# ScalarE moments, a wider row spacing and a shared c/d bank in a Winograd-tiled attention and FFN kernel

## The chip, the cores and the metric

The kernel runs on one core of a Trainium2 chip. Its engines run side by side, each with a queue of its own that is worked off in order: TensorE (PE, with PEld for its weight loads), VectorE (DVE), ScalarE (ACT), GpSimd (POOL) and SyncE (SP), whose queue issues nearly all DMAs. An instruction that has to wait for another engine holds up everything behind it in its queue. The metric is the time of one execution in microseconds (us) on the device; the time before is 2470.33 us, the median of three runs from 2461.07 to 2472.49.

## The reference

The input is x with 8 sequences of 512 rows of 1024 numbers, all float32. Two blocks follow each other, each with a layer norm in front of it and one behind it, and a residual sum:

```python
x = x + _layernorm(attn(_layernorm(x), Wq, Wk, Wv, Wo))       # causal attention, 16 heads of 64, rotary
x = x + _layernorm(ffn(_layernorm(x), weight, bias, lora_A, lora_B, starts))

def _layernorm(x, axis=-1, eps=1e-05):
    m = jnp.mean(x, axis=axis, keepdims=True)
    v = jnp.var(x, axis=axis, keepdims=True)
    return (x - m) / jnp.sqrt(v + eps)
```

`ffn` is one 1024 x 1024 linear layer with a low-rank adapter that is chosen for each sequence. So each sequence meets a projection with Wo, a norm of the result, the sum with x, a norm of that sum, the projection with the FFN weight, a norm and a sum.

## The kernel before

**Three stages.** The first (V) projects the eight sequences with Wv, the second does the query and key products and the attention, the third does sixteen projections: q = 0 to 7 are the eight sequences with Wo, q = 8 to 15 the same with the FFN weight. The first and third stages use one scheme, class `Group` and `products` (L295 to L391), and the change lies there.

**Tiling.** A matrix product is done by two nested levels of Strassen-Winograd: seven outer products P1 to P7 (`GROUPS`, in the order `ORDER`), each of seven inner products (`SUBS`, in the order `SLOTS`). An inner product is two matmuls of 128 x 128 by 128 x 256 in the code, and one inner product is one *tick*. A projection takes N2 = 49 ticks. The inner products of a group add into four accumulators in PSUM, named a, b, c and d, each 128 x 256 float32. `SLOTS` says in which order within a group: slot 0 opens b (P6), slot 1 opens a (P1), slot 2 adds the last product P3 of the *group before* into that group's c, slot 3 opens c (P5), slot 4 opens d (P4), slot 5 adds to b (P7), slot 6 adds to a (P2).

**Drains.** One tick after a product, its `drain` (L339) takes the results out: after slot 1, ACT copies a to `p1` (L347) and DVE forms `u2` from b and `p1`; after slot 5, DVE adds b into `p1` and adds c and d to it (three adds, L342); after slot 6, ACT copies a (L354); after slot 2, DVE adds c to `u2`. PE may add to b in slot 5 only when DVE has read it for `u2`, and `u2` needs ACT's copy. PE may add P3 to c in slot 2 of the next group only when DVE has read c.

**Buffers.** PSUM has eight banks. `ACCS` (L79) gives one, two, two and one buffers to a, b, c and d, with two for a when q >= 0; each buffer takes a bank of its own, though it fills half of one. In V two more banks hold transposes, in the third stage one holds the adapter's products.

**Order.** It is written out by hand. `at(tick, fn)` puts an event on a tick; `run` issues at each tick the product, then the drain of the product before, then the events of that tick in the order in which they were put there. With base = 49 q, the events of projection q at `base + k` that matter here are these. Sums of the outer products (L275 to L277): at k = 45 DVE adds A to U and at 46 U to c22 (one instruction of 128 x 1024 each), at 48 c22 to c12, at 52 A to c22; POOL adds to c21 at 38 and 47. Operands of the next projection (`plan_right`, L1167): loads of R11, R21, R12, R22 at 10, 17, 24, 31 on SP's queue, then T1 at 38, T2 at 45, T4 at 52 and T3 at 63 on POOL (three subtractions each); for q >= 8 T1 and T3 are DVE's.

**Rows.** `plan_rows` (L1203) treats the result of a projection in four row tiles t of 128 rows, seven ticks apart, starting at k = 55 + 7 t, that is during the next projection. For a tile: load the residual row (k); `stats` in four steps at k, k+1, k+3, k+4, which are `bn_stats` on the two halves and `bn_aggr` on DVE, a square root on ACT, reciprocal and the factor `nb` on DVE; two `norm` passes on ACT (k+6, k+7, L420); two adds of the residual on POOL (k+8, k+9, L1124); a store (k+14). For q < 8 the norm of the sum follows, with `stats` on DVE at k+14 to k+18 (key x), two `norm` passes at k+20 and k+21, two transposes on DVE at k+24 and k+25 (`turn_x1`, L1133) and eight small stores. Tiles 0 and 1 are c11 and c21, tiles 2 and 3 are c22 and c12. The residual rows take three buffers with tag `row` and one with tag `lb`; `lb` also holds the adapter's output matrix, which POOL fetches by an indirect DMA (`pick_b`, L1090).

Of the kernel before, what the change touches and what calls it, by code (L numbers as in the profile page):

```python
# [10 lines left out]
F32 = mybir.dt.float32  # L11
I32 = mybir.dt.int32
AF = mybir.ActivationFunctionType
# [4 lines left out]
P = 128  # L18
# [7 lines left out]
HALF = 512  # L26
# [37 lines left out]
SUB = 256  # L64
# [11 lines left out]
SLOTS = ["P6", "P1", "P3", "P5", "P4", "P7", "P2"]  # L76

QK = {"P1": "A", "P2": "B", "P6": "D", "P7": "E", "P4": "F", "P5": "D", "P3": "E"}
ACCS = {"a": 1, "b": 2, "c": 2, "d": 1}  # L79
SLOT_L = {"L11": 0, "L12": 1, "S3": 2, "L22": 3, "S1": 4, "S2": 5, "S4": 6}  # L80
SLOT_R = {"R11": 0, "R21": 1, "T3": 2, "R22": 3, "T1": 4, "T2": 5, "T4": 6}

# [51 lines left out]
def sandwich_kernel(  # L134
# [58 lines left out]
    def at(tick, fn, kind=None):  # L193
        events[tick].append((kind, fn) if kind else fn)
# [100 lines left out]
    class Group:  # L295
# [9 lines left out]
        def product(self, p):  # L305
            l, r, a = SUBS[p]
            first = a not in self.acc
            if first:
                self.acc[a] = env["acc"].tile(
                    [P, SUB], F32, tag=a, bufs=2 if a == "a" and self.q >= 0 else ACCS[a], name=f"acc{a}_{self.name}"  # L310
                )
            acc = self.acc[a]
            left, right = self.W[self.L], RX[self.q, self.R][:, SLOT_R[r]]
            for k in range(2):
                stays = right[:, k, :] if self.q < B else by_blocks(right, k)
                if self.q < 0:
                    moving = left[:, SLOT_L[l], k, :]
                else:
                    moving = left[:, 4 * k : 4 * k + 4, SLOT_L[l], :]
                nc.tensor.matmul(  # L320
                    acc, lhsT=stays, rhs=moving,
                    start=(first and k == 0), stop=True, skip_group_check=True,
                )
            if self.lora and p in LORA_SUB:
                half, cols = self.lora
                i, c = LORA_SUB[p]
                nc.tensor.matmul(
                    acc, lhsT=hts[self.q - B][:, cols[c], :],
                    rhs=env["lb"][self.q - B][:, half * HALF + i * SUB : half * HALF + (i + 1) * SUB],
                    start=False, stop=True, skip_group_check=True,  # L330
                )
# [7 lines left out]
        def drain(self, p):  # L339

            acc, t = self.acc, self.t
            add = lambda out, x, a: nc.vector.tensor_tensor(out, acc[a], x, op=ALU.add)  # L342
            if p == "P1":
                env["u2"].reverse()
                for n, pool in (("p1", env["p1"]), ("u2", env["u2"][0])):
                    t[n] = pool.tile([P, SUB], F32, tag=n, name=f"{n}_{self.name}")
                nc.scalar.copy(t["p1"], acc["a"])  # L347
                add(t["u2"], t["p1"], "b")
            elif p == "P7":
                add(t["p1"], t["p1"], "b")  # L350
                add(self.dest(1, 1), t["p1"], "c")
                add(self.dest(1, 0), t["p1"], "d")
            elif p == "P2":
                nc.scalar.copy(self.dest(0, 0), acc["a"])  # L354
            elif p == "P3":
                add(self.dest(0, 1), t["u2"], "c")
# [38 lines left out]
    def stats(key, srcs, step):  # L395
        small = env["small"]
        if step == 0:
            ln[key] = small.tile([P, 2, 6], F32, tag="bnst", name=f"bn_{key}")
        if step < 2:
            nc.vector.bn_stats(ln[key][:, step, :], srcs[step])  # L400
        if step == 1:
            mv = small.tile([P, 2], F32, tag="mv", name=f"mv_{key}")
            nc.vector.bn_aggr(mv, ln[key])
            ln[key] = mv
        if step == 2:
            mv = ln[key]
            sd = small.tile([P, 1], F32, tag="sd", name=f"sd_{key}")
            nc.scalar.activation(sd, mv[:, 1:2], AF.Sqrt, bias=eps, scale=1.0)
            ln[key] = mv, sd
        if step == 3:  # L410
            mv, sd = ln[key]
            rs = small.tile([P, 1], F32, tag="rstd", name=f"rstd_{key}")
            nc.vector.reciprocal(rs, sd)
            nb = small.tile([P, 1], F32, tag="nb", name=f"nb_{key}")
            nc.vector.tensor_scalar(nb, mv[:, 0:1], rs, -1.0, op0=ALU.mult, op1=ALU.mult)
            ln[key] = rs, nb

    def norm(key, dst, src):
# [647 lines left out]
    with ExitStack() as a:  # L1066
# [5 lines left out]
        ps_p = a.enter_context(tc.tile_pool(name="ps_p2", bufs=1, space=PSUM))  # L1072
        ps_t = a.enter_context(tc.tile_pool(name="ps_t2", bufs=1, space=PSUM))
        env.update(acc=ps_p, cp=cp, p1=tl, u2=[tl, tmp], small=small)

# [12 lines left out]
        def pick_b(b):  # L1090
            lb[b] = (rows if b % 2 else lc).tile([P, E], F32, tag="lb", bufs=1, name=f"lb_{b}")
            pick(lb[b], lora_b, 1, b)
# [19 lines left out]
        def load_row(q, t):  # L1112
            if (q, t) == (NQ - 1, 3):
                row[q, t] = lc.tile([P, E], F32, tag="lb", bufs=1, name=f"row_{q}_{t}")
            elif q < B and t == (3 if q + 1 < B else 0):
                row[q, t] = rows.tile([P, E], F32, tag="lb", bufs=1, name=f"row_{q}_{t}")
            else:
                row[q, t] = rows.tile([P, E], F32, tag="row", bufs=3, name=f"row_{q}_{t}")
            src = x[q, ts(t, P), :] if q < B else x1d[q - B][:, t, :]
            nc.sync.dma_start(out=row[q, t], in_=src)  # L1120
# [46 lines left out]
        def plan_right(q, base):  # L1167

            if q > 1:
                at(base + 6, next_roles)  # L1170
            for n, k in (("R11", 10), ("R21", 17), ("R12", 24), ("R22", 31)):
                if q == 1 and n != "R22":
                    continue
                at(base + k, lambda n=n: load_right(gp, q, n))
                if q >= B:
                    at(base + k + 4, lambda n=n: sub_right(q, n, nc.gpsimd, slice(0, 3)))
            if q >= B:
                for h, k in ((0, 25), (1, 39)):
                    at(base + k, lambda h=h: lora_in(q - B, h), "pe")
                    at(base + k, lambda ph, h=h: lora_keep(q - B, h, ph), "post")  # L1180
                    for g in range(2):
                        at(base + k, lambda n=f"R{g + 1}{h + 1}": sub_right(q, n, nc.vector if h else nc.gpsimd, slice(3, 4)))
                at(base + 42, lambda: sub_ht(q - B))
                if q - B:
                    at(base + (10 if q - B > 1 else 33), lambda: pick_b(q - B))
                if q + 1 < NQ:
                    at(base + 43, lambda: pick_a(q - B + 1))
            for n, k in (("T1", 40 if q == 1 or q >= B else 38), ("T2", 46 if q >= B else 45), ("T4", 52), ("T3", 63)):
                eng = nc.vector if q >= B and n in ("T1", "T3") else nc.gpsimd
                for m in range(3):  # L1190
                    at(
                        base + k + (m if eng is nc.vector else 0),
                        lambda n=n, m=m, eng=eng: sum_right(gp, q, n, eng, slice(m, m + 1)),
                    )
# [8 lines left out]
        def plan_rows(q, base):  # L1203

            for t in range(NT):
                k = base + 55 + 7 * t
                key = f"{'o' if q < B else 'y'}{q}_{t}"
                at(k, lambda t=t: load_row(q, t))
                for m in range(4):
                    at(k + m + m // 2, lambda t=t, m=m, key=key: stats(key, halves(q, t), m))  # L1210
                for h in range(2):
                    at(k + 6 + h, lambda t=t, h=h, key=key: norm(key, halves(q, t)[h], halves(q, t)[h]))
                    at(k + 8 + h, lambda t=t, h=h: add_row(q, t, h))
                at(k + 14, lambda t=t: store_rows(q, t))
                if q < B:
                    key = f"x{q}_{t}"
                    for m in range(4):
                        at(k + 14 + m + m // 2, lambda t=t, m=m, key=key: stats(key, halves(q, t), m))
                    for h in range(2):
                        at(k + 20 + h, lambda t=t, h=h, key=key: norm(  # L1220
                            key, row[q, t][:, ts(h, HALF)], halves(q, t)[h]
                        ))
                    for g in range(2):
                        at(k + 24 + g, lambda t=t, g=g: turn_x1(q, t, g))
                        at(k + 29 + g, lambda t=t, g=g: store_x1(q, t, g))
# [172 lines left out]
```

## Time and profile before

| what | value | how to read it |
|---|---|---|
| median of the runs | 2470.33 us | three runs, 2461.07 to 2472.49 |
| profiled execution | 2470.53 us | its own time |
| its span | 2468.4 us | first to last instruction |
| PE busy | 2356.1 us, 95% | so PE idles 112.3 us in all |
| DVE, ACT, POOL busy | 73%, 42%, 62% | averages over stages that differ |
| projections 1 to 5, mean length | 44.8 us | from 1749.9 to 1974.1 us, five of them, cut at their longest waits |
| of such a projection (1838.3 to 1883.3) | DVE 40.33, ACT 18.76, POOL 38.07 us busy | of 45.00 us |

The page has one line for each group of instructions: line of the code, engine, operation, output and input with their shapes, count, busy time and mean duration, then the idle time of the engine just before. The timeline gives for each instruction its start, its length, its engine and line, and in square brackets how long the engine had been idle and what released it.

### The profile page before, as it was taken

The numbers are of one execution on the slowest core, as the hardware profiler recorded it, in microseconds if no ns is written. First come the engines' busy times: TensorE is split into PE (matmuls) and PEld (weight loads), VectorE is DVE, ScalarE is ACT, GpSimd is POOL, SyncE is SP. The second block draws the span as 40 slices with busy tenths as digits, with TensorE's granted clock in tenths as the row PEclk, the third lists the DMA queues.
The fourth block names the chain that finished last, engine by engine and source line by source line (L and its number), as shares of the span: only waits on it lengthen the run. The fifth ranks groups of instructions, "written<-read, shape, count | busy, mean of one in ns | idle before, by whom it ended". The sixth has DMA issues, their size and how long they took to land.

```text
span 2468.4 us, 37185 instructions
## 1 busy us (share of the span) xinstructions
PE 2356.1 (95%) x11936; PEld 1858.0 (75%) x11936; DVE 1790.1 (73%) x3946; ACT 1045.4 (42%) x2650; POOL 1535.8 (62%) x1139
## 2 busy tenths in 40 slices
PE   6999999999999999999999999899999988999997
PEld 4887887886677777777777776558888867888886
DVE  8777767485857759577595866776899888776676
ACT  3323331025555555555555566652434433222223
POOL 4878875204363553735646364776887886777874
PEclk8999999999999999999999999899999999999999
DMA  7697787998899897989889897467777788545443
GB/s 264 196 302 247 245 269 230 353 304 265 269 298 291 248 340 239 312 297 292 314 259 341 265 303 245 135 230 261 241 213 233 216 261 246 136 144 148 139 122 119
DMA packets 506016, 606.47 MB, mean 246 GB/s; under 512 B 197600, under 2 KB 344032, under 8 KB 503264
## 3 DMA queue, kind: packets, MB, share of 16 engines
q1 hardware_dynamic: 504288, 598.87, 76.7%
q0 software_dynamic: 1536, 5.24, 0.7%
q8 instruction: 96, 1.57, 0.3%
q14 instruction: 96, 0.79, 0.1%
HBM read 371.20 MB, written 199.23 MB: 231 GB/s over the span
## 4 chain that ended last, share of the span: by engine, by line
PE 65%; DVE 6%; DMA 5%; POOL 2%; ACT 2%; issue 1%; SPq 1%; ACTq 0%; DVEq 0%; POOLq 0%
PE accb_q_P L641 7%; PE acca_q_P L641 7%; PE accc_q_P L641 7%; PE accc_P L320 6%; PE accb_P L320 6%; PE acca_P L320 6%; PE s L753 6%; PE po L835 6%; PE ptp L814 5%; PE accd_q_P L641 3%; PE accd_P L320 3%; DMA wo_d<-wc_wo 1%; DVE U L360 1%; ACT pr L784 1%; DMA attn<-opt 1%
## 5 line engine op out<-in xcount | busy, mean ns | idle before, releaser
L784 ACT ACTIVATE pr<-pr,nm 128x128 f32<-128x128 f32 (+3 forms) x512 | 281.0, 550 | 188.4 <-DVE nm L774 188.2
L800 ACT ACTIVATE pr<-pr,rs 128x128 f32<-128x128 f32 x470 | 231.0, 550 | 109.4 <-DVE rs L792 109.3
L774 DVE CUSTOM_DVE_ANT_0 pr<-s,mask 128x128 f32<-128x128 f32 (+3 forms) x512 | 224.2, 484 | 43.1 <-PE s L753 41.1
L641 PE MATMUL acca_q_P<-xs,ls 128*128 128x256 f32 x896 | 217.3, 385 | 0.8 <-DMA ls<-wqk 0.8
L641 PE MATMUL accc_q_P<-xs,ls 128*128 128x256 f32 x896 | 217.1, 385 | 0.0
L641 PE MATMUL accb_q_P<-xs,ls 128*128 128x256 f32 x896 | 216.3, 384 | 0.8 <-DVE u_q_P L117 0.8
L1124 POOL TENSOR_TENSOR c<-c,row 128x512 f32<-128x512 f32 x120 | 161.8, 1357 | 88.4 <-ACT c L420 73.2
L641 PEld LDWEIGHTS acca_q_P<-xs,ls 128*128 128x128 f32 x896 | 165.3, 190 | 49.9 <-issue 19.4
L641 PEld LDWEIGHTS accc_q_P<-xs,ls 128*128 128x128 f32 x896 | 165.3, 190 | 48.2 <-issue 20.2
L641 PEld LDWEIGHTS accb_q_P<-xs,ls 128*128 128x128 f32 x896 | 165.4, 190 | 44.9 <-issue 6.6
L753 PE MATMUL s<-qk 64*128 64x128 f32 (+3 forms) x1024 | 192.5, 472 | 4.4 <-DVE nm L774 4.2
L814 PE MATMUL ptp<-ident,pr 128*128 128x128 f32 x1280 | 178.7, 278 | 12.8 <-DVE nm L774 5.9
L814 PEld LDWEIGHTS ptp<-ident,pr 128*128 128x128 f32 x1280 | 147.6, 142 | 44.8 <-ACT pr L800 15.9
L275 POOL TENSOR_TENSOR T<-R,T 128x512 f32<-128x512 f32 (+1 forms) x96 | 171.3, 1812 | 14.2 <-PE accc_P L320 9.6
L567 POOL TENSOR_TENSOR wc_g<-wc_g 128x256 f32<-128x256 f32 (+1 forms) x120 | 127.0, 1077 | 79.6 <-DMA wc_g<-in_wqk_dram 76.3
L835 PE MATMUL po<-pT,v 128*64 128x512 f32 (+3 forms) x1024 | 157.6, 446 | 8.2 <-ACT pT L829 6.1
L835 PEld LDWEIGHTS po<-pT,v 128*64 128x64 f32 x1024 | 72.8, 138 | 100.1 <-issue 66.2
L684 POOL TENSOR_TENSOR B_q<-B_q,m 128x1024 f32<-128x1024 f32 x14 | 33.1, 2368 | 175.7 <-DVE B_q L681 175.7
L641 PE MATMUL accd_q_P<-xs,ls 128*128 128x256 f32 x448 | 108.8, 386 | 0.4 <-DVE p_q_P L117 0.4
L829 DVE COPY pT<-ptp 128x384 f32<-128x384 f32 (+1 forms) x132 | 80.4, 614 | 39.3 <-PE ptp L814 39.2
L753 PEld LDWEIGHTS s<-qk 64*128 64x128 f32 x1024 | 73.1, 186 | 44.7 <-issue 28.7
L567 POOL TENSOR_TENSOR wc_wo<-wc_wo 128x256 f32<-128x256 f32 (+1 forms) x64 | 66.0, 1049 | 64.2 <-DMA wc_wo<-in_wo_dram 50.8
(1120 smaller groups left out, 5750.6 us busy)
## 6 DMA issues: line engine op xcount, KB each, us to landing
ls<-wqk SPq DMA_DIRECT2D x392, 256.0 KB, 5.3
xs<-xop SPq DMA_DIRECT2D x392, 256.0 KB, 5.4
R<-attn SPq DMA_DIRECT2D x32, 896.0 KB, 6.4
wqk<-wc_g SPq DMA_DIRECT2D x16, 1568.0 KB, 9.4
x<-in_x_dram SPq DMA_DIRECT2D x32, 512.0 KB, 9.7
v<-vd SPq DMA_DIRECT2D x64, 256.0 KB, 5.4
attn<-ops SPq DMA_DIRECT2D x16, 1024.0 KB, 7.7
row<-in_x_dram SPq DMA_DIRECT2D x32, 512.0 KB, 5.4
```

What stands on the lines that cost most here:

```text
L275: eng.tensor_tensor(RX[q, n][:, c], RX[q, x][:, c], RX[q, y][:, c], op=ALU.subtract)
L320: nc.tensor.matmul(acc, lhsT=stays, rhs=moving, start=(first and k == 0), stop=True, skip_group_check=True,)
L567: eng.tensor_tensor(out, x, y, op=op)
L641: nc.tensor.matmul(acc[:, :, w, :], lhsT=ls[:, k, w, :], rhs=xs_[:, :, k, :], start=(first and w == 0 and k == 0), stop=True, skip_group_c ...
L753: nc.tensor.matmul(ps[:, j, at : at + L], lhsT=qT[r, qb], rhs=kT[r, : qb + 1], start=True, stop=True,)
L774: nc.vector.tensor_tensor_reduce(out=v[:, j, :], in0=self.ps[qb][:, j, :], in1=work2["mask"][:, S - L :], scale=-1.0 / HD**0.5, scalar=3.0e38,
L784: nc.scalar.activation(v[:, j, :], v[:, j, :], AF.Exp, bias=nm[:, j : j + 1], scale=-1.0, accum_out=sm[:, j : j + 1],)
L800: nc.scalar.mul(v, v, rs[:, j : j + 1])
L814: nc.tensor.transpose(pt[:, n, :], self.pr[qb][:, j, ts(kb, P)], ident)
L829: copy(self.pT[j][:, : qb + 1, ts(qb, P)], self.pt[j][:, : qb + 1, :])
L835: nc.tensor.matmul(po[j * HD : (j + 1) * HD, kb * P :], lhsT=self.v[:, kb, ts(j, HD)], rhs=self.pT[j][:, kb, kb * P :], start=(kb == 0), s ...
L1124: nc.gpsimd.tensor_tensor(c, c, row[q, t][:, ts(h, HALF)], op=ALU.add)
```

## The change

The moments (mean and variance) of the *first* norm behind the Wo projection (key o, q < 8) are no longer computed by `stats` on DVE but by a new function `moments`, by ACT passes whose elementwise results go to a spare PSUM bank called `unread` that nobody reads; only their running sums are used. The row tiles of q < 8 are nine ticks apart instead of seven. The accumulators c and d are two halves of one tile of one bank, with two buffers, and a has two buffers in every stage, V included. With this `first` is false for d, so only c's first matmul carries the start flag. In the drain after slot 5, d is read before c. For the last q < 8 the `lb` buffer goes to tile 1 instead of tile 0, and one fetch moves from tick 33 to 42.

```diff
-ACCS = {"a": 1, "b": 2, "c": 2, "d": 1}
...
-            if first:
-                self.acc[a] = env["acc"].tile(
-                    [P, SUB], F32, tag=a, bufs=2 if a == "a" and self.q >= 0 else ACCS[a], name=f"acc{a}_{self.name}"
-                )
+            if a in "ab" and first:
+                self.acc[a] = env["acc"].tile([P, SUB], F32, tag=a, bufs=2, name=f"acc{a}_{self.name}")
+            elif a == "c" and first:
+                both = env["acc"].tile([P, 2, SUB], F32, tag="c", bufs=2, name=f"accc_{self.name}")
+                self.acc["c"], self.acc["d"] = both[:, 0], both[:, 1]
...
             elif p == "P7":
                 add(t["p1"], t["p1"], "b")
+                add(self.dest(1, 0), t["p1"], "d")
                 add(self.dest(1, 1), t["p1"], "c")
-                add(self.dest(1, 0), t["p1"], "d")
...
+    def moments(key, srcs, junk, step):
+
+        small, act, n = env["small"], nc.scalar.activation, len(srcs)
+        if step == 0:
+            nm = small.tile([P, 2], F32, tag="nm", name=f"nm_{key}")
+            for i, v in enumerate(srcs):
+                act(junk[:, : v.shape[-1]], v, AF.Identity, scale=-1.0 / E, accum_out=nm[:, i : i + 1])
+            if n > 1:
+                act(nm[:, 0:1], nm[:, 0:1], AF.Identity, bias=nm[:, 1:2], scale=1.0)
+            ln[key] = nm
+        if step == 1:
+            sq = small.tile([P, 2], F32, tag="sq", name=f"sq_{key}")
+            for i, v in enumerate(srcs):
+                act(junk[:, : v.shape[-1]], v, AF.Square, bias=ln[key][:, 0:1], scale=1.0, accum_out=sq[:, i : i + 1])
+            ln[key] = ln[key], sq
+        if step == 2:
+            nm, sq = ln[key]
+            sd = small.tile([P, 1], F32, tag="sd", name=f"sd_{key}")
+            if n > 1:
+                act(sq[:, 1:2], sq[:, 1:2], AF.Identity, bias=eps, scale=1.0 / E)
+            act(sd, sq[:, 0:1], AF.Sqrt, bias=sq[:, 1:2] if n > 1 else eps, scale=1.0 / E)
+            ln[key] = nm, sd
+        if step == 3:
+            nm, sd = ln[key]
+            rs = small.tile([P, 1], F32, tag="rstd", name=f"rstd_{key}")
+            nc.vector.reciprocal(rs, sd)
+            nb = small.tile([P, 1], F32, tag="nb", name=f"nb_{key}")
+            act(nb, nm[:, 0:1], AF.Identity, scale=rs)
+            ln[key] = rs, nb
...
+        unread = ps_t.tile([P, HALF], F32, tag="unread", bufs=1, name="unread")
...
-            elif q < B and t == (3 if q + 1 < B else 0):
+            elif q < B and t == (3 if q + 1 < B else 1):
...
-                    at(base + (10 if q - B > 1 else 33), lambda: pick_b(q - B))
+                    at(base + (10 if q - B > 1 else 42), lambda: pick_b(q - B))
...
-                k = base + 55 + 7 * t
+                k = base + 55 + (9 if q < B else 7) * t
...
-                    at(k + m + m // 2, lambda t=t, m=m, key=key: stats(key, halves(q, t), m))
+                    at(k + m + m // 2, lambda t=t, m=m, key=key: (
+                        moments(key, halves(q, t), unread, m) if q < B else stats(key, halves(q, t), m)
+                    ))
```

## The prediction

> **What bounds the kernel now.** I read the page's slices first, then PE's waits, then the timelines of all engines around the longest of these waits.
>
> ```profile
> PE   6999999999999999999999999899999988999997
> ACT  3323331025555555555555566652434433222223
> ```
>
> PE is full nearly everywhere, ACT is the emptiest engine. Time can be won only where PE waits; here are all waits behind the first Wo projection that the change touches, and one of V's:
>
> ```profile
> PE accc_P L320 <- DVE A L342: 20.1, 9, 4.2
> PE accb_P L320 <- DVE u_P L342: 3.7, 2, 2.1
> PE acca_-6_P L320 <- ACT A_-6_1100 L354: 0.8, 1, 0.8
> ```
>
> Six of the nine waits for c are in projections 1 to 6, once in each: 11.0 us together, 1.83 us each. Two of 4.2 and 3.4 us are in q = 7 and 8, with both waits for u (2.1 and 1.6). The place, in PE's timeline (second line; the others are from V):
>
> ```profile
> 142.56 1.13 PE L320 MATMUL acca_-6_P<-wv_L,R_-6_839 128*128 128x256 f32 x4 [0.75 <-ACT A_-6_1100 L354]
> 145.62 0.66 PE L454 MATMUL ptx<-ident,x 128*128 128x128 f32 x4 [0.20 <-ACT x L420]
> ...
> 1794.18 1.13 PE L320 MATMUL accc_P<-wo_S,R 128*128 128x256 f32 x4 [1.94 <-DVE A L342]
> ```
>
> Products start 0.864 us apart (eleven from 1780.86 to 1790.36). The one at 1794.18 is tick 51 of its projection: P3 into c, which DVE must have read. DVE's own timeline shows why it has not:
>
> ```profile
> 1787.61 0.38 DVE L342 TENSOR_TENSOR U<-accc_P,u_P 128x256 f32<-128x256 f32 x1
> ...
> 1788.82 2.30 DVE L360 TENSOR_TENSOR U<-U,A 128x1024 f32<-128x1024 f32 x1
> 1791.16 2.17 DVE L360 TENSOR_TENSOR c<-c,U 128x1024 f32<-128x1024 f32 x1
> 1793.26 0.41 DVE L342 TENSOR_TENSOR p_P<-accb_P,p_P 128x256 f32<-128x256 f32 x1
> 1793.70 0.42 DVE L342 TENSOR_TENSOR A<-accc_P,p_P 128x256 f32<-128x256 f32 x1
> 1794.05 0.41 DVE L342 TENSOR_TENSOR A<-accd_P,p_P 128x256 f32<-128x256 f32 x1
> ...
> 1796.02 0.41 DVE L342 TENSOR_TENSOR u_P<-accb_P,p_P 128x256 f32<-128x256 f32 x1
> ```
>
> Between the last U drain (tick 45) and c stand two wide sums of 4.5 us. No `bn_stats` of key o is in this stretch: those that go were at ticks 55 to 80.
>
> **DVE at ticks 45 to 54.** A tile's relief is 2 x 0.67 + 0.21 + 0.21 = 1.8 us (`bn_stats`, `bn_aggr`, `nb`), 7 us for each projection, but elsewhere. What matters is what the nine-tick spacing puts here: tile 3's x statistics come at 47 and 48 (were 41, 42), tile 2's transposes at 48 and 49 (were 44, 45). I walk through DVE's new order, with distances between starts from the same timeline. The U drain now starts when its product ends, 1787.13, as no transpose is ahead of it. Then drain 0.46, U 2.34, c22 2.10, one `bn_stats` 0.60, b 0.44, d 0.35: c is read from 1793.42 to 1793.83, and PE resumes 0.06 later, at 1793.89. It could have at 1792.24: the wait is 1.65 instead of 1.94, in spite of d being read first, which costs 0.35. But u of the next group, which PE needs at tick 54, now stands behind a transpose (0.62), `bn_stats` (0.71), `bn_aggr` (0.12), the c12 sum (1.64) and a second transpose (0.62): it starts at 1793.76 + 3.71 = 1797.47 and ends at 1797.89. PE would be there at 1793.89 + 2.70 = 1796.59, so it waits 1.36 us. Sum 3.0 us a projection, against 1.83.
>
> **ACT.** The rows for a pass:
>
> ```profile
> L784 ACT ACTIVATION_READ_ACCUMULATOR pr<-pr,nm 128x1 f32 x512 | 95.9, 187 | 0.0
> L784 ACT ACTIVATE pr<-pr,nm 128x512 f32<-128x512 f32 x128 | 91.4, 714 | 139.6 <-DVE nm L774 139.4
> L420 ACT ACTIVATE c<-c,nb_o,rstd_o 128x512 f32<-128x512 f32 x64 | 49.9, 803 | 15.9 <-DVE nb_o L415 15.9
> L408 ACT ACTIVATE sd_o<-mv_o,eps 128x1 f32<-128x1 f32 x32 | 9.5, 296 | 12.6 <-DVE mv_o L403 12.6
> ```
>
> A running sum adds a read of 0.19, of which 0.09 stands out. A second operand by partition costs 0.09 (0.803 against 0.714), so Identity, which has none, is 0.62 + 0.09 and Square 0.71 + 0.09. All four passes of a tile write the same `unread`, so each waits for the one before to end: 0.03 more (the gap that dependent DVE instructions show). That makes 0.74 and 0.83; four small instructions of 0.33 follow. A tile is 2 x 0.74 + 2 x 0.83 + 4 x 0.33 = 4.5 us, and one root of 0.3 goes: 16.6 us more for each projection on an engine with 18.8 busy in 45: 79%. It fits on average. But ACT must also copy a (L347) on time: from slot 1 it has about 2.6 us until PE stops at slot 5. At 61 that just holds (0.15 us). From 61 to 89 nothing loosens the row of tiles 0 (norm), 1, 2 and 3: I add ACT's queue up from tile 3's old x norm at 1798.2. The copy before tick 61 ends at 1803.7; then tile 0's rest with its norms (to 1807.2), a copy, tile 1 with two copies (to 1814.1), tile 2 with tile 0's x norm (1.42) and copies (to 1822.7), tile 3 with tile 1's x norm (to 1828.8), the copy for group 5 to 1829.15, u to 1829.65. PE reaches that slot, tick 89, at 1804.2 + 28 x 0.864 = 1828.4. It waits 1.2 us. If a pass took only 0.60 and 0.70 and a small one 0.2 (no wait among them), 3.7 us less stand ahead of that copy, and nothing is late; at the norm's rate (0.803 + 0.12 for all) 2 us more are. So ACT costs 0 to 3.6 us a projection; I take 1.35, nearest to the rows of L784. The spare destination could make a pass shorter; no row shows it.
>
> By the Trainium skill, "ScalarE: Activation LUTs", section "What ACT_TABLE_LOAD costs", an immediate pass is 186 ns + 0.833 ns an element and each pointer operand adds 93 ns: 0.61 and 0.71 us, as the rows say. Its section "Rules for kernel authors" says to use VectorE, not ScalarE, for adds and multiplies; that speaks against the change: a half-row that took DVE 0.67 takes ACT 1.6. Were all of it on the path, 32 tiles x 2.4 would be 77 us; by the queues above only what is late counts.
>
> **POOL.**
>
> ```profile
> 1779.41 2.68 POOL L1124 TENSOR_TENSOR c<-c,row 128x512 f32<-128x512 f32 x2 [4.54 <-ACT c L420]
> 1782.05 4.30 POOL L275 TENSOR_TENSOR T<-R,R 128x512 f32<-128x512 f32 x3
> 1786.30 2.52 POOL L360 TENSOR_TENSOR c<-c,c 128x512 f32<-128x512 f32 x2
> 1788.76 6.25 POOL L275 TENSOR_TENSOR T<-R,T 128x512 f32<-128x512 f32 x3
> 1794.96 3.49 POOL L360 TENSOR_TENSOR c<-c,U 128x512 f32<-128x512 f32 x2
> 1798.42 5.26 POOL L275 TENSOR_TENSOR T<-R,T 128x512 f32<-128x512 f32 x3
> ```
>
> Tile 3's residual adds move from ticks 35, 36 to 41, 42, behind T1 and the first c21. T1 can't start before PE is through tick 37 (1781.0), which frees its buffer, so POOL's stretch to the end of T4 becomes 4.25 + 2.46 + 2.64 + 6.20 + 3.46 + 5.23 = 24.24 and ends at 1805.3. PE wants T4 at tick 63, now 1805.9. So the adds are just covered, by PE's own waits: without them PE would be there at 1802.6 and wait 2.7 us for POOL. This is what comes late next.
>
> **New waits between engines.** DVE's `bn_stats` at tick 47 waits for POOL's first add: done at 1781.0 + 4.25 + 2.46 + 1.35 = 1789.1, DVE is there at 1792.0. That add waits for ACT's norm of tile 3, at tick 42 or so; POOL is there at 1787.7, tick 46. ACT's pass over c21 at tick 56 waits for POOL's second c21 sum (1800.1); ACT is there at 1800.4, with the copy for tick 58 behind it and DVE's u behind that: half a microsecond of POOL's lateness would reach PE at 61. DVE's reciprocal of key o now waits for a root at the end of ACT's passes, with the next drains behind it; at tick 59 the root is 0.4 us ahead.
>
> **The rest.** V: the 0.75 us for a's one buffer goes, but DVE has no gap from 131.37 to 145.2 there, and its reciprocal for x releases ACT's norm at 144.75 and the transposes at 145.62: these would wait 0.95 instead of 0.20. Nothing won; if that cover fails, 0.8 x 6 = 4.5 us. d ahead of c lies ahead of the same transposes; for q > 8 PE waits only once for c after 2100 us (1.5 us), so 0.35 is covered there. q = 7 and 8: one `bn_stats` (0.7) leaves the stretch before tick 47, so I take 0.7 off each wait for u: -1.4. What tick 51 gains there tick 54 gives back, as above. ACT's lateness hits q = 7 too (+1.3); in q = 8 adapter products make the projection 61.6 us long and cover it. SP: each tile's residual load, two stores and eight small stores issue 0, 2, 4 or 6 ticks later; tile 3's small stores pass the load of R11, and R21 behind them lands in 6.4 us with some 30 ticks to go. The moved fetch (0.97 us on POOL) has 3.4 us until T4 is wanted in q = 8. Without that cover it costs its 1 us. A table load for Sqrt stays one.
>
> **Sum.** Six projections: 3.0 + 1.35 - 1.83 = 2.5 each, 15.1; q = 7 and 8: -0.1. The profiled execution took 2470.53 us with a span of 2468.4, 0.2 from the median, so 2470.5 + 15 = 2485.5. Its own bounds: ACT at nothing +7 and at its highest +29; V off 4.5; contention a few either way: 2473 to 2501.
>
> **Rivals.**
> - *ACT becomes the bound.* At the upper pass cost the lateness (3.6 a projection) also delays tile 3's norm, POOL's adds and T2. For it: 79% on average, in order. Against it: Identity has an operand less than the exponential's row. 7 x (3.0 + 3.6 - 1.83) = +33: 2504.
> - *Even.* ACT on time, and DVE's new wait at 54 half hidden: within 6 us of before. For it: a few tenths decide at 54. 2472.
> - *Faster, by the wide sums.* c12's sum took 1.21 us at 2030.66 and the U sum 4.13 at 2024.23, while POOL worked. If POOL's shifted order leaves DVE its sums at 1.22, the three at 45 to 48 shrink from 6.1 to 3.7, PE's 3.0 to 0.6, and T2 and T4 to the 4.3 of other projections. With ACT on time, 6 x 1.2, and 3.6 in each of q = 7 and 8: -14, 2456. It decides from a sum of the three below 4.9 us. Against it: POOL's stretch is without gaps.
>
> On that sharing the Trainium skill ("SBUF — State Buffer", "SBUF: two separate sides") says that a DVE operation with two SBUF inputs and a GpSimd operation lock each other out whole; `bn_stats` has one input, so by the rule its leaving frees no lock.
>
> **Chances.** Forecast 0.50, ACT as bound 0.16, even 0.14, faster 0.20. Within 0.5% (about what this kernel's measurement can tell) means 2458 to 2482.7: even, and the low end of the forecast (0.06). Faster 0.19, same 0.21, slower 0.60. The range for 8 in 10: 2457 to 2504.
>
> **What would show it.** PE's waits in projections 1 to 6: c at tick 51 of about 1.6, a new one for u at tick 54 of 1.4, one for u at tick 40 (89) behind ACT's p copy. Identity near 0.62, Square near 0.71. V's transposes waiting 0.9. Wrong if the three sums run near 1.2, if ACT's passes overlap, or if PE waits for POOL's T4.

## The result, and the profile after

The changed kernel takes 2500.88 us (median of four runs, 2496.62 to 2507.11), the kernel before beside it 2469.02 us (four runs, 2461.07 to 2472.49): a ratio of 1.0133, 95% interval 1.0114 to 1.0153. It is slower by 31.9 us, where the forecast said 15. The profiled execution took 2507.11 us, with a span of 2505.0; it is the slowest of the four.

The slices of ACT on the page of the changed kernel:

```profile
ACT  3323321026555555555565565645677654222222
```

and, from the view of PE's waits, the longest that lie behind the first Wo product (line, what it waited for; total us, times, longest):

```profile
PE accb_P L320 <- DVE u_P L342: 23.0, 15, 6.6
PE accc_P L320 <- DVE A L342: 11.1, 7, 1.8
PE ph L1184 <- DMA R<-x1t: 9.8, 3, 5.8
PE accc_P L320 <- DVE U L342: 8.5, 10, 3.0
```

ACT works more in the Wo stage, as it should: 5 to 7 tenths in slices 28 to 33, which had 2 to 4. The wait for c (`DVE A`) is down from 20.1 to 11.1 us. But waits for u rise from 3.7 to 23.0, those of the adapter's product `ph` for its operands R, which are loaded from `x1t`, from 5.0 to 9.8, and a wait for U is new.

Where does the time go? I cut each trace at two products that are in both: the first of the Wo stage, and tick 51 of q = 6.

| stretch | before | after | difference |
|---|---|---|---|
| start to the first Wo product | 1676.67 | 1682.77 | +6.1 |
| projections: from there to tick 51 of q = 6 | 297.42 | 311.58 | +14.2 |
| last stretch: from there to the end | 494.31 | 510.65 | +16.3 |

The first row is mostly scatter. Four of the runs below have the changed kernel's code up to there and reach that product at 1674.9, 1676.6, 1677.7 and 1678.9 us; five kernels with the code of before reach it at 1672.2 to 1676.7. The second row is firm: in these four runs the projections take 311.55 to 311.57 us. The cut of this row holds six waits at tick 51 and five at tick 54, so I also give five whole periods, from tick 51 of q = 1 to tick 51 of q = 6: 226.1 us before, 238.8 after, 2.5 us more for each projection. Of the third row's 16.3 us, 8.7 lie between tick 51 of q = 8 and tick 51 of q = 9 (62.4 us against 53.7).

A projection of the changed kernel, the timeline of PE (start, length, instruction, then the idle time ahead of it and what ended it):

```profile
1838.98 1.13 PE L320 MATMUL accb_P<-wo_S,T 128*128 128x256 f32 x4 [0.62 <-DVE u_P L342]
...
1843.07 1.13 PE L320 MATMUL accc_P<-wo_S,T 128*128 128x256 f32 x4 [0.37 <-DVE U L342]
...
1851.03 1.13 PE L320 MATMUL accc_P<-wo_S,R 128*128 128x256 f32 x4 [1.64 <-DVE A L342]
...
1855.45 1.13 PE L320 MATMUL accb_P<-wo_L,R 128*128 128x256 f32 x4 [1.56 <-DVE u_P L342]
```

They are ticks 40, 44, 51 and 54: 4.2 us of waits in a period of 47.8 us (1803.27 to 1851.03), where there were 1.9. The drain of u for tick 40 needs ACT's copy of a to `p1` (L347). ACT's timeline shows what stands ahead of that copy: the last pass of tile 3 (L431), a norm of tile 1 (L450) and, not shown, the read of the running sum, another copy of a and two small instructions of tile 3.

```profile
1835.20 0.69 ACT L431 ACTIVATE unread<-c,nm_o 128x512 f32<-128x512 f32 x1
...
1836.18 1.52 ACT L450 ACTIVATE row<-c,nb_x,rstd_x 128x512 f32<-128x512 f32 x2
...
1838.11 0.35 ACT L347 COPY p_P<-acca_P 128x256 f32<-128x256 f32 x1
```

For ticks 51 and 54, DVE's timeline shows what stands ahead of c and u, the sums into U and c12. The first line is POOL's, the residual adds of tile 3:

```profile
1843.47 2.50 POOL L1155 TENSOR_TENSOR c<-c,row 128x512 f32<-128x512 f32 x2
1844.70 2.35 DVE L360 TENSOR_TENSOR U<-U,A 128x1024 f32<-128x1024 f32 x1
...
1852.33 2.14 DVE L360 TENSOR_TENSOR c<-c,c 128x1024 f32<-128x1024 f32 x1
...
1855.02 0.38 DVE L342 TENSOR_TENSOR u_P<-accb_P,p_P 128x256 f32<-128x256 f32 x1
```

And the timeline in q = 8, of POOL, DVE and PE, where the largest part of the last stretch's loss sits:

```profile
2113.46 0.95 POOL L1112 DMA_INDIRECT la<-in_lora_a_dram,picks  x1 [0.30 <-issue]
2114.43 4.27 POOL L274 TENSOR_TENSOR T<-R,T 128x512 f32<-128x512 f32 x3
2118.65 2.48 POOL L360 TENSOR_TENSOR c<-c,U 128x512 f32<-128x512 f32 x2
2121.10 4.23 POOL L274 TENSOR_TENSOR T<-R,T 128x512 f32<-128x512 f32 x3
...
2117.32 9.10 DVE L360 TENSOR_TENSOR c<-c,c 128x1024 f32<-128x1024 f32 x1
...
2127.40 2.08 PE L320 MATMUL accb_P<-wf_L,R 128*128 128x256 f32 x4 [6.64 <-DVE u_P L342]
```

DVE's sum into c12, an instruction of 1.2 us when alone (1.21 at 2030.66 before), takes 9.10. It ends 1.09 us after the last of POOL's subtractions (2121.10 + 4.23 = 2125.33; 2117.32 + 9.10 = 2126.42). So it stood still until POOL's run of subtractions and sums was through, and then ran. The drain of u is behind it, and PE waits 6.64 us. The four matmuls that follow take 2.08 us instead of 1.13: the granted clock from 2127.4 to 2132.0 us is 0.50.

### The profile page after: what moved, and what is told of

It is laid out like the page before. It is cut to its first block, busy times and chain, and to the rows that moved or that the text cites. A ratio compares the mean times of both kernels' runs of the same rounds, so it can differ in the third digit from the quotient of the medians.

```text
span 2505.0 us, 37353 instructions
## 1 busy us (share of the span) xinstructions
PE 2367.4 (95%) x11936; PEld 1858.5 (74%) x11936; DVE 1748.6 (70%) x3818; ACT 1159.1 (46%) x3002; POOL 1525.9 (61%) x1139
## 4 chain that ended last, share of the span: by engine, by line
PE 63%; DVE 8%; DMA 5%; ACT 3%; SPq 2%; issue 1%; POOL 1%; ACTq 0%; DVEq 0%; POOLq 0%
PE accc_P L320 8%; PE accb_q_P L671 7%; PE accc_q_P L671 7%; PE acca_q_P L671 7%; PE s L783 6%; PE po L865 6%; PE accb_P L320 5%; PE acca_P L320 5%; PE ptp L844 5%; PE accd_q_P L671 3%; DVE c L360 2%; DMA xs<-xop 1%; PE accc_P L327 1%; SPq L254 1%; DVE c L1164 1%
## 5 line engine op out<-in xcount | busy, mean ns | idle before, releaser
L342 DVE TENSOR_TENSOR u_P<-accb_P,p_P 128x256 f32<-128x256 f32 x109 | 45.6, 418 | 107.0 <-ACT p_P L347 106.4
L262 POOL TENSOR_TENSOR R<-R 128x256 f32<-128x256 f32 x96 | 73.2, 762 | 58.2 <-DMA R<-x1t 47.6
```

What stands on the lines that cost most here:

```text
L262: eng.tensor_tensor(t[:, out], t[:, x], t[:, y], op=ALU.subtract)
```

## The experiments

Every run has runs of the kernel before beside it (those of one batch share them), and the ratio refers to these. "Projections" and "last stretch" are cut from the one profiled execution as above; runs 6 and 11 have no wait at tick 51 and are cut at tick 58 of q = 6, in the text.

| run | ratio to before, 95% interval | projections | last stretch |
|---|---|---|---|
| kernel before | 1 | 297.4 | 494.3 |
| changed kernel | 1.0133 (1.0114 to 1.0153) | 311.6 | 510.7 |
| 1 bank alone | 1.0030 (1.0016 to 1.0044) | 298.2 | 494.3 |
| 2 nine ticks alone | 1.0076 (1.0059 to 1.0093) | 296.3 | 506.7 |
| 3 passes and bank, seven ticks | 1.0060 (1.0043 to 1.0077) | 308.7 | 498.9 |
| 4 changed, R21 ahead of the stores | 1.0118 (1.0101 to 1.0135) | 311.6 | 513.3 |
| 5 changed, c12's sum later | 1.0130 (1.0111 to 1.0149) | 311.6 | 511.8 |
| 6 before, sums behind the drains | 1.0002 (0.9991 to 1.0014) | | |
| 7 run 4, fetches behind T4 | 1.0130 (1.0110 to 1.0150) | 311.6 | 508.2 |
| 8 bank and nine ticks, no passes | 1.0066 (1.0045 to 1.0087) | 296.8 | 512.3 |
| 9 before, la behind T4 | 0.9993 (0.9983 to 1.0003) | 297.6 | 494.5 |
| 10 run 4, la behind T4, lb at 41 | 1.0093 (1.0075 to 1.0110) | 311.6 | 498.7 |
| 11 runs 6 and 9 together | 0.9994 (0.9984 to 1.0004) | | |
| 12 changed, tile 3 by DVE | 1.0085 (1.0070 to 1.0100) | 298.7 | 516.3 |

**1. The bank alone.** The kernel before with the hunks on `ACCS`, `acc` and the order of d and c.

> The kernel before with only the bank part: c and d in one bank, two buffers of every accumulator, d read ahead of c; statistics by DVE, row tiles seven products apart. Theory (the bank part costs a few tenths, since c is read 0.35 us later at tick 51 of each projection): the wait for c there goes from 1.83 to about 2.2 us, the time to 2468 to 2474. Rival A (two buffers of a and d free PE where it waited): a gain over 3 us, below 2466. Rival B (sharing the bank makes PE wait for two readers at other places, V's 896 products among them): new waits of PE for c outside tick 51, above 2480.

2473.89 us. The wait at tick 51 is 2.27 instead of 1.92, as the theory has it, and the last stretch is unchanged. The stage V is no faster and no slower: the next stage starts at 430.4 us, in kernels with four banks at 429.1 to 431.8. The ratio says 4 to 11 us, the trace accounts for less than 1. The profiled execution was the fastest of the six runs, so where the rest lies stays open. In the nine profiles with the shared bank the first Wo product comes at 1676.8 us on average, in the five with four banks at 1674.0; the ranges overlap, so this is no more than a hint.

**2. Nine ticks alone.**

```diff
-                k = base + 55 + 7 * t
+                k = base + 55 + (9 if q < B else 7) * t
```
(with the moved fetch and `lb` row of the change)

> The kernel before with only the order part: row tiles nine products apart for the projection, the moved fetch and row buffer; statistics by DVE, four separate banks. Theory (the order costs most of what the change lost: DVE's order at ticks 45 to 54, and in q = 7 and 8 the order on SP): a wait for u at tick 54 of 1.5 to 2.2 us in each projection beside 1.2 to 1.7 at tick 51, waits of the adapter's product for R21 of 3 to 6 us in q = 7 and 8: 2485 to 2495. Rival (ScalarE's passes make the loss, the order alone nothing): 2465 to 2473.

2485.23 us, as expected in sum, but not in its place. The projections lose nothing: waits of 0.40 at tick 51, 1.36 at 54 and 0.47 for T4 replace 1.9, and five whole periods take 226.7 us against 226.1 (the 1.2 us gained in the table come from where the cut lies). All of the loss, 12.4 us, is in the last stretch, with a wait of 8.65 us for u in q = 8 behind a c12 sum of 9.75 us.

**3. Passes and bank at seven ticks.** The changed kernel with the lines of run 2 undone.

> The changed kernel with row tiles seven products apart again (passes by ScalarE and one bank kept). Theory (the passes need the nine ticks: 4.5 us of passes, 3.0 of norms and 0.7 of copies are 8.2 us a tile against 6.05 us of products): ScalarE falls behind by 2 us a tile, PE waits for u behind its p copies by 4 to 9 us in each projection, 2500 to 2535, but the last stretch (q = 7 and 8) has no wait over 4 us for R21. Rival (the nine ticks are what lost the time): 2465 to 2480.

2483.70 us, between the two ranges; the expected size of ACT's lateness was too large, but the place is right. PE waits 1.78 us for u, once in each projection, at tick 33, and 1.74 at tick 51; the projections lose 11.3 us. The last stretch loses 4.6. So with the rows at seven ticks the last stretch is nearly spared, and the projections lose all the same.

**4. R21 ahead of tile 3's stores.** Hypothesis: SP's queue is what made q = 7 and 8 slow. In q = 8 and 9 R21 reads x1t, the adapter's product needs it at tick 25, and the load (tick 17) stood behind stores (ticks 13, 14) that wait for DVE.

```diff
-                        at(k + 29 + g, lambda t=t, g=g: store_x1(q, t, g))
+                        at(k + (34 if t == 3 else 29) + g, lambda t=t, g=g: store_x1(q, t, g))
```

> The changed kernel with the small stores of each projection's tile 3 issued five ticks later, so behind the load of R21 on SP's queue instead of ahead of it. Theory (in q = 7 and 8 R21 is late since its load stands behind these stores, which wait for DVE's transposes): the waits of 3.7 and 5.8 us for R21 fall below 1.5 each, and with them part of the 9 us of low clock and the 9.1 us wide sum behind them: 2485 to 2495. Rival A (another wait takes their place, or the store behind is late for its reader): 2497 to 2504. Rival B (R21 waits for its buffer or its source, not for the queue): the waits stay, 2497 to 2504.

2498.26 us, rival A. PE's waits for R21 at tick 25 fall from 3.71 and 5.84 to 0.26 us in all. But R12 and R22, needed at tick 39, are now waited for (6.6 us, the longest 2.88), and the c12 sums of q = 7 and 8 take 10.90 and 9.77 us, and PE waits 10.32 and 8.75 us for u. What stands first in the queue hid what stands second.

**5. The c12 sum behind u.**

```diff
-                (48, dve, "c12", "c12", "c22"), (52, dve, "c22", "c22", "A"),
+                (52, dve, "c12", "c12", "c22"), (52, dve, "c22", "c22", "A"),
```

> The changed kernel with only DVE's sum into c12 moved from tick 48 to tick 52 of its projection, so behind the drain of u that PE wants at tick 54. Theory (PE's wait for u is DVE's order: the 2.14 us sum, 9.10 us in q = 8, stands ahead of a 0.4 us drain): the waits for u of 1.56 fall below 0.4 in the projections, the 6.6 us wait in q = 8 below 3, at most half of it coming back at the next drain: 2486 to 2493. Rival (DVE has no slack there, the wait goes whole to the c drain of tick 55): PE waits 1.2 us or more for c at tick 58, 2496 to 2503.

2500.72 us, the rival. In the timeline of PE the wait for u is gone, and tick 58 has one of the same size:

```profile
1855.23 2.86 PE L320 MATMUL accc_P<-wo_L,R 128*128 128x256 f32 x12 [1.75 <-DVE A L342]
```

What is moved behind one drain is ahead of the next. In the last stretch c12's sums are short now (1.68 and 1.89 us), and yet it stays at 511.8: the U sum of q = 8 starts while POOL issues a fetch and takes 5.58 us, PE waits 9.7 us for R, and the projections from q = 10 on are 0.7 to 0.9 us longer each.

**6. A try: sums behind the drains, in the kernel before.** c22 + U from 46 to 49, c12 + c22 from 48 to 52, c22 + A from 52 to 53, tile 3's transposes from k+24 to k+27.

> A try at a faster kernel, from the kernel before: in every group of sums U + A stays at tick 45, c22 + U goes from 46 to 49 (behind the drains of A), c12 + c22 from 48 to 52 and c22 + A from 52 to 53 (behind u and the last drain of A), tile 3's transposes three ticks later. Theory (PE's wait of 1.9 at tick 51 is DVE's order, as the forecast read it): the wait for c at tick 51 falls below 0.4 in the projections, waits of up to 0.8 come up at tick 54 or 58, and 4.2 and 3.4 us in q = 7 and 8 fall to 3 and 2: 2454 to 2463. Rival (DVE is short of time in the stretch, any order hands the wait on): 2464 to 2472.

2468.59 us: no change, the rival. The wait moved as in run 5: tick 51 has none, tick 58 one of 1.0 to 1.5 us. From the first Wo product to tick 58 of q = 6 that is 298.5 us against 303.6, but from there to the end 492.2 against 488.1, with 4.8 us of wait for R21 in q = 8.

**7. The fetches behind T4.** In the runs so far every DVE sum that was shut out for longer than one instruction met a run of POOL that began with T2 right behind an indirect fetch.

```diff
-                    at(base + (10 if q - B > 1 else 42), lambda: pick_b(q - B))
+                    at(base + (10 if q - B > 1 else 53), lambda: pick_b(q - B))
-                    at(base + 43, lambda: pick_a(q - B + 1))
+                    at(base + 53, lambda: pick_a(q - B + 1))
```
(on top of run 4)

> The changed kernel with tile 3's small stores behind the load of R21 (as in the run of that edit, 2498.3) and GpSimd's indirect fetches of the adapter rows moved from ticks 42 and 43 to 53, so from ahead of T2 to behind T4. In the runs so far a DVE sum was shut out through several GpSimd instructions (4.1 to 10.9 us) only where an indirect fetch stood right ahead of T2; in the projections, without such a fetch, it got in after one instruction (2.1 us). Theory A (the fetch ahead of T2 is what lets GpSimd keep the port): the sums into c12 in q = 7 and 8 take 1.2 to 2.4 us instead of 10.9 and 9.8, the waits for u there fall from 10.3 and 8.8 to under 3: 2478 to 2488. Rival B (GpSimd's backlog alone does it, whatever stands ahead): sums of 8 us or more stay in both, 2493 to 2502.

2498.79 us, and still theory A is right on what it names: the sums take 2.13 and 1.33 us, the waits for u are 1.56 and 0.32. The time went into a new wait, PE's timeline in q = 9:

```profile
2128.51 1.19 PE L327 MATMUL accc_P<-lb,htb 128*128 128x256 f32 x2 [8.07 <-DMA lb<-in_lora_b_dram,picks]
```

lb, fetched at 2122.73, is needed at 2120.4. Run 10 puts that right.

**8. Bank and nine ticks without the passes.** The kernel before with the edits of runs 1 and 2.

> The changed kernel with the statistics of the results by DVE again (bn_stats), so the bank and the nine ticks without ScalarE's passes. Theory (the parts add up, and ScalarE's passes cost the projections through the copies that come late and the U sum that slips): projections like the run with the nine ticks alone plus 0.35 at tick 51 (waits of 0.7 and 1.4, no wait for u at tick 40), the last stretch as slow as there: 2484 to 2492. Rival (the passes cost nothing once nine ticks are there; the bank and the order together make the loss): 2496 to 2504, with a wait of 1.6 at tick 51.

2486.01 us, as the theory has it: waits of 0.73 at tick 51, 1.03 at 54, 0.47 for T4, none at 40, a period of 45.3 us. DVE's U sum is short here, as it starts ahead of POOL's residual adds (two from 1832.22, which take 4.47 us instead of 2.50):

```profile
1831.93 1.42 DVE L360 TENSOR_TENSOR U<-U,A 128x1024 f32<-128x1024 f32 x1
```

The projections take 296.8 us; the changed kernel differs by the passes only and takes 311.6. So the passes cost the projections 14.8 us. For the last stretch this pair says little (512.3 against 510.7): both c12 sums are shut out here (10.88 and 9.75 us), in the changed kernel only that of q = 8.

**9. la behind T4, in the kernel before.** One line of run 7, `pick_a` at 53.

> The kernel before with only GpSimd's indirect fetch of the next adapter's rows (la) moved from tick 43 to tick 53, behind T4. Theory (the fetch right ahead of T2 shuts DVE's sum of U + A out, 4.13 us in q = 7 and 8, and PE's waits of 4.2 and 3.4 us for c hang on it): both sums take 1.2 to 2.4 us, the two waits fall by 1.5 to 2 us each, with a little clock: 2462 to 2466. Rival (T2 and DVE would collide as much without the fetch): sums of 4 us stay, 2467 to 2470.

2463.74 us. The sums of U + A fall from 4.13 and 4.14 to 1.36 us each, the c22 sums behind them grow from 1.23 to 2.72, the waits for c from 4.21 and 3.36 to 2.94 and 2.07. So the theory holds for the sums, and the waits fall by 1.3 us each. The stretch is as long as before (494.5 against 494.3), with 2.99 us of wait for R21 in q = 8 where there were 1.5. No gain can be told from none.

**10. la behind T4, lb early enough, in the changed kernel.** Run 4, `pick_a` at 53, and `pick_b` for the second sequence at 41, between two residual adds.

> The changed kernel with tile 3's small stores behind R21, la fetched at tick 53, and the one moved fetch of lb at tick 41 (between the two residual adds) instead of 53, where the 8.1 us wait for it came from. Theory (the shut-out sums in q = 7 and 8 are what the last stretch lost most by): no wide sum there over 2.4 us, no wait for lb over 1 us, the last stretch, from tick 51 of q = 6 to the end, within 4 us of the kernel before (494), the projections unchanged: 2484 to 2491. Rival (a fetch two adds ahead of T2 does the same): the c12 sum of q = 8 takes 8 us or more, 2491 to 2497.

2488.91 us. The last stretch takes 498.7 us instead of 510.7, 4.4 above the kernel before. The timelines of POOL and DVE in q = 7, first of run 4, with the fetch ahead of T2:

```profile
2044.07 0.97 POOL L1112 DMA_INDIRECT la<-in_lora_a_dram,picks  x1
2045.06 4.26 POOL L274 TENSOR_TENSOR T<-R,T 128x512 f32<-128x512 f32 x3
...
2046.13 10.90 DVE L360 TENSOR_TENSOR c<-c,c 128x1024 f32<-128x1024 f32 x1
```

and of run 10, without it:

```profile
2042.76 5.26 POOL L274 TENSOR_TENSOR T<-R,T 128x512 f32<-128x512 f32 x3
...
2045.02 1.32 DVE L360 TENSOR_TENSOR c<-c,c 128x1024 f32<-128x1024 f32 x1
```

In both, DVE's sum starts while POOL is in T2. With the fetch ahead it waits for T2, c21 and T4; without it, it gets in after one instruction, and T2 takes 1.0 us longer instead (5.26 for 4.26). It is not a matter of the moment: in q = 8 of run 2 the sum starts 1.00 us into T2's second subtraction, with the fetch ahead of T2, and takes 9.75 us; here it starts 1.03 us into the second subtraction and takes 1.32. The table of windows (busy us of PE, PEld, DVE, ACT, POOL, then PE's granted clock, DMA share and GB/s) for 1980 to 2140 us, of the kernel before, the changed kernel and run 10:

```profile
1980.00:2140.00 160.00, 143.66 (x693) 119.36 (x692) 128.11 (x257) 49.35 (x100) 117.26 (x100) 0.98 0.83 237
```

```profile
1980.00:2140.00 160.00, 133.35 (x597) 109.45 (x596) 115.58 (x212) 77.99 (x188) 111.91 (x89) 0.91 0.75 218
```

```profile
1980.00:2140.00 160.00, 140.85 (x666) 116.44 (x664) 117.36 (x231) 78.04 (x189) 119.62 (x95) 0.97 0.81 234
```

The clock falls to 0.91 with the long waits and comes back to 0.97 without them: it is a part of what a wait costs here.

**11. Runs 6 and 9 together.** The likeliest candidate against both kernels.

> The kernel before with the sums behind the drains (as in the run of that order, 2468.6) and la fetched at tick 53: the likeliest to beat both kernels. Theory (the two gains add up): 2459 to 2465, wide sums below 2.4 us in q = 7 and 8. Rival (the order of the sums gives nothing, the fetch alone counts): the same time as the kernel before with the fetch alone moved, within 2 us.

2464.04 us, the same as run 9, as the rival has it; but it lies in the theory's range too, and no wide sum in q = 7 and 8 is over 2.18 us, so the two can't be told apart. In its one profile the first Wo product to tick 58 of q = 6 takes 298.4 us and the rest 488.1, against 303.6 and 488.1 before; the times of the eleven runs show no such 5 us. It is faster than the changed kernel, but no gain over the kernel before can be told.

**12. Tile 3 by DVE.**

```diff
-                        moments(key, halves(q, t), unread, m) if q < B else stats(key, halves(q, t), m)
+                        moments(key, halves(q, t), unread, m) if q < B and t < 3 else stats(key, halves(q, t), m)
```

> The changed kernel with the statistics of tile 3 of each projection by DVE (bn_stats), of tiles 0 to 2 by ScalarE's passes. Theory (the passes cost only where a copy of a comes late, at tick 40, and by what that shifts): the waits of 0.62 at tick 40 and 0.38 at 44 vanish, those at ticks 51 and 54 fall from 1.65 and 1.56 to about 0.7 and 1.0, as with no passes at all, the period from 47.8 to 45.3 to 46: 2485 to 2491. Rival (each tile's passes cost their share, so a quarter of 14.8 us comes back): 2495 to 2500.

2487.53 us, the theory. The waits at ticks 40 and 44 are gone, one of 0.35 us at tick 61 is new, and PE's timeline at ticks 51 and 54 reads:

```profile
1836.25 1.13 PE L320 MATMUL accc_P<-wo_S,R 128*128 128x256 f32 x4 [0.53 <-DVE A L342]
...
1840.13 1.13 PE L320 MATMUL accb_P<-wo_L,R 128*128 128x256 f32 x4 [1.02 <-DVE u_P L342]
```

The projections are back at 298.7 us. Three tiles of passes cost the projections 2 us (298.7 against run 8's 296.8), the fourth 13. The U sum is short again (1.24 us). No run took out another tile than tile 3, so it isn't shown whether its place or the load of a fourth tile decides. The time does not come back whole, as the c12 sums of q = 7 and 8 are shut out for 10.89 and 12.12 us here (last stretch 516.3).

## Why the forecast was right, and where it was not

**The time lies in the range, but by luck.** 2500.88 us is 0.1 us below the upper end of 2473 to 2501. That end stood for ACT at its highest cost (+29), and ACT's passes did not cost that. More than half of the loss, 16.3 us, lies where the forecast had -0.1.

**Projections: the waits and the sum are right, the split between the causes is not.** 15.1 us were forecast for q = 1 to 6, 14.2 were measured. Step by step:

- *c at tick 51 and u at tick 54*: 1.65 and 1.36 forecast, 1.64 and 1.56 measured. The walk through DVE's queue gives the right waits from the durations of neighbouring rows. But the split was wrong. The order was to cost 1.2 us a projection and the passes 1.35. Run 8 shows that order and bank together cost nothing (296.8 against 297.4), and the passes 2.5 us (14.8 in six). The link is the U sum: 2.35 us with the passes (1844.70), where it starts during POOL's residual adds (1843.47) and ends 1.08 us after them, and 1.42 in run 8, where it starts ahead of them. The forecast took 2.34 from the kernel before as if it were a property of the sum. That the passes brought it back to this length made the sum of the two parts come out, and that was luck.
- *ACT*: one Identity pass to the next takes 0.74 to 0.82 us (0.74 forecast), one Square to the next 0.85 (0.83). The lateness at tick 40 was 1.2 by the forecast; measured are 1.22 at its first place and 0.62 to 0.64 at the others, with 0.38 at tick 44 that it did not name. Run 12 shows that these and what they shift hang on tile 3's passes.
- *POOL*: PE waits nowhere for T4 in the changed kernel, as forecast, and does in runs 2 and 8, where its own waits are shorter, by 0.47 and not by the 2.7 that were named.
- *V*: nothing won, as forecast. The wait for a (0.75 us at 142.56) went to c (0.64 at 143.80) and not to the transposes.

**q = 7 and 8: the step that failed.** The forecast put them at -0.1 us. The last stretch lost 16.3. Its text said "What tick 51 gains there tick 54 gives back, as above" and took DVE's sums there to be as long as in the projections. The nine ticks move a transpose, the second `bn_stats` and `bn_aggr` to the place ahead of c12's sum (2115.88 to 2117.40 us in q = 8), so that it starts when T2, c21 and T4 stand ready on POOL. In the projections it waits for one POOL instruction at most (2.14 us). In q = 8 of the changed kernel, where the fetch of la is right ahead of T2, it waits for all of them (9.10 us), and so do seven more sums in runs 2, 4, 8 and 12 (9.8 to 12.1 us). Runs 4, 7 and 10 show it: the fetch moved, the sum is short. The sign was on the page of before: the forecast itself quoted the U sum of 4.13 us at 2024.23, but as a matter of sharing, without asking what POOL had done just ahead.

**SP: a slip.** "R21 ... lands in 6.4 us with some 30 ticks to go" holds for q = 2 to 7. In q = 8 and 9 the adapter wants R21 eight ticks after the load is issued, and PE waited 3.71 and 5.84 us. Run 4 took these two away, got 6.6 us of waits for R12 and R22 for them, and won nothing that can be told (ratios 1.0118 and 1.0133, intervals that overlap), with both c12 sums shut out behind them.

**The moved fetch of lb** was priced at 1 us on POOL if its cover failed. In the changed kernel, where it stands ahead of la and T2 in q = 8, PE has no wait for lb. Moved on to tick 53 in run 7 it cost 8.07 us, as there its landing time counts.

**What is left.** 14.2 and 16.3 make 30.5 of the 31.9 us. Run 10 gives back 12 in the last stretch, run 12 gives back 13 in the projections; no run had both. Run 10's last stretch is still 4.4 us above the kernel before. In it PE waits 11.7 us for R from `x1t`, where the kernel before waits 5.0, so what is left may well lie in these loads; no run tested that. Why DVE's sum stands still behind a fetch is open, too: in two profiles (the changed kernel and run 2, both in q = 7) the c12 sum took only 2.15 and 2.14 us although a fetch stood there; in both, a DVE sum was in flight when T2 began, and T2's three subtractions took 4.54 and 4.53 us instead of 4.27. And in q = 8 of run 10, where the fetch of lb is right ahead of a residual add, the U sum got in after that one add (2.56 us). So every sum that was shut out had a fetch right ahead, but not every sum with a fetch ahead was shut out.

## What to carry to other kernels

Average load of an engine says little about moving work to it: three tiles of four cost 2 us on ACT, the fourth 13, and the trace shows it ahead of one small copy that PE needs. Ask of a stage that looks like the others (here q = 7 and 8) which instructions only it has, and walk the queues there with these; a duration that is long beside a neighbour's is a wait, and the question is for what. When a wait is removed and the time stays, look for the next one in the same queue: of the twelve runs, five only moved a wait.

## What the hardware showed that was not expected

A DVE sum with both operands in SBUF normally gets in after one GpSimd instruction: 2.14 us for c12's in the projections of the changed kernel, where a subtraction of T2 in turn takes 2.24 instead of 1.27 us. Right behind an indirect fetch, GpSimd ran up to eight instructions in a row at full speed (4.27, 2.48 and 4.23 us) and DVE stood still for all of them: eight sums of 9.1 to 12.1 us in q = 7 and 8 over the runs, and of 4.1 to 5.6 us where only T2 stood ready. With no fetch right ahead of T2 (runs 7, 9, 10 and 11) none there was over 2.72. The Trainium skill ("SBUF — State Buffer", section "SBUF: two separate sides") says that whichever of the two starts first has the shared ports for the whole instruction and blocks the other. One instruction is what the projections show. The 9.10 us span the rest of one and five whole GpSimd instructions, so here the sum did not get in at the end of an instruction, and the measurement decides.
